# Cross-attention over a long context: a projection in 64-row pieces copied out by two engines, and layer 0's maxima taken over pairs of key blocks with the mask worked into the keys by GpSimd

## The chip, the cores and the metric

The kernel runs on one core of one Trainium2 chip. The time is device microseconds from the start to the end of one execution. Engines are named as in the profile: PE is TensorE's matrix product, PEld its weight load, DVE is VectorE, ACT is ScalarE, POOL is GpSimd, SP is SyncE, which here only issues DMAs.

## The reference

Four layers, each a cross-attention over a context of 12544 tokens of 192 numbers, a self-attention and a feed-forward block of experts, on 128 query tokens of width 256. The change concerns the cross-attentions of layers 0, 1 and 2 (16 heads of 16 numbers; layer 3 has 64 to a head and is written otherwise). Layer 0:

```python
q = (x @ Wq).reshape(B, N, HEADS, hd).transpose(0, 2, 1, 3)
k = (context @ Wk).reshape(B, M, HEADS, hd).transpose(0, 2, 1, 3)
v = (context @ Wv).reshape(B, M, HEADS, hd).transpose(0, 2, 1, 3)
scores = jnp.einsum('bhid,bhjd->bhij', q, k) * scale
scores = jnp.where(context_mask[:, None, None, :], scores, max_neg)
attn = jax.nn.softmax(scores, axis=-1)
out = jnp.einsum('bhij,bhjd->bhid', attn, v)
return out.transpose(0, 2, 1, 3).reshape(B, N, DIM) @ Wo
```

Layers 1 and 2 add biases to q, k and v and have no mask; layer 1 clips the scores at 10000 and replaces the weights by a mean if any score is not a number. All arithmetic is fp32. In the inputs the mask is true everywhere, but the kernel computes with whatever mask it is given.

## The kernel before

The context is cut into 25 blocks of 512 tokens (NSB), the last of 256. Keys and values are projected from it per group `g` of eight heads (two groups in layers 0 to 2), so the context is read once for each group. `Net.context` loads a block ahead: rows 0 to 127 of the transposed context into a tile `ctxA` (128 x 512) and the other 64 rows into `ctxB`, whose two halves of 256 tokens lie in partitions 0 to 63 and 64 to 127.

`Keys.project(g, b, low)` projects block `b` in two parts. With `low` = 0 the products contract over 128 rows (keys: two products of 256 columns, values: four of 128 x 128); with `low` = 1 over the last 64 rows, where the two halves of the block use the upper and the lower half of TensorE's rows. All add into one pair of PSUM banks (`pair`), keys in the first 256 columns of each bank and values in the others. Then ScalarE copies keys (L131, L133 with bias) and values (L137) to SBUF, both halves in one instruction. Each fp32 product appears in the trace as two records of PE and two of PEld. The first blocks of layers 1 and 2 (EARLY = 8) are projected before the layer, while the experts of the layer before run.

`attend_twice_in` goes over the keys twice for each group. The first pass finds the maximum of every query's scores; the second computes exponentials less that maximum and adds up the weighted values. In PSUM there are four pairs of banks (`ppr=4`) that all products of the first pass take in turn, so a product waits until the pair taken four products earlier has been read.

- First pass, layers 1 and 2, "by twos": for blocks 2i and 2i+1, GpSimd makes the difference of the two blocks of keys (`apart`, L570). The scores of the difference go through a relu on ScalarE (`over`, L578), the scores of block 2i+1 are added and the maximum taken by one fused VectorE instruction (`highest_of_two`, L586), since max(a, b) = relu(a - b) + b. A round `b` of the loop does this for one half `s` of the heads' pairs: it projects a block two ahead, makes the scores of the difference, and finishes the maximum of the round before.
- First pass, layer 0 (masked): for each block and `s`, TensorE first writes the mask's row into PSUM by a bf16 product with ones (L558), adds the scores (L559), and VectorE takes the maximum over each bank (`highest`, L565). The mask's rows come into SBUF by four small DMAs a block from SP (L547).
- Second pass: scores (L629), exponentials (L654, L677, L692), weighted values (L699). For layer 0 GpSimd issues four small DMAs of mask rows a block (L547), of which the products read two.

Order: `in_order` binds the instructions of PE, DVE and ACT in a loop to the order in which they are written. GpSimd and SP, whose instructions here are DMAs, differences and sums, are ordered by the scheduler, each in one queue that is worked off in order.

In layer 1 GpSimd also adds up all context columns (`add_up`, L99, L100) for the case of scores that are not numbers. `load_mask` reads the mask and makes its rows and columns. `load_kv` loads a weight of 192 rows: 128 rows once, and the other 64 twice, for both halves of the partitions. The layer-3 attention (`KeysInTurn`, `attend_once_in`) uses the same context tiles with loads two blocks ahead.

Of the kernel before, what the change touches and what calls it, by code (L numbers as in the profile page):

```python
# [12 lines left out]
F32 = mybir.dt.float32  # L13
BF16 = mybir.dt.bfloat16
# [10 lines left out]
CB = CD - P  # L25
H = 16
# [27 lines left out]
class Keys:  # L54
# [4 lines left out]
    def __init__(self, net, wk, wv, groups, bias=None, sums=None):  # L59
        self.net, self.nc, self.wk, self.wv, self.bias, self.sums = net, net.nc, wk, wv, bias, sums  # L60
        self.context = net.context(groups * NSB)
        self.started, self.done, self.rest = {}, 0, None
        if sums is not None:
            self.nc.gpsimd.memset(sums, 0.0)
# [30 lines left out]
    def add_up(self, g, b):  # L95
        if g == 0 and self.sums is not None:
            a, c = self.context(b)
            n = HB * len(self.halves(b))
            self.nc.gpsimd.tensor_tensor(self.sums[:, :n], self.sums[:, :n], a[:, :n], ALU.add)  # L99
            self.nc.gpsimd.tensor_tensor(self.sums[:, SB:], self.sums[:, SB:], c, ALU.add)  # L100
# [16 lines left out]
    def values_into(self, p, g, low, blocks, first=0, turn=None):  # L117
        cols = slice(g * P, g * P + P)
        for j, b in enumerate(blocks):
            ctx = self.context((g if turn is None else turn) * NSB + b)[low]  # L120
            for c in range(2):
                for i, r in self.halves(b):
                    at = first + (2 * j + c) * P
                    r = r if low else slice(0, P)
                    k = c * P if low else i * HB + c * P
                    self.mm(p[:, i, at : at + P], ctx[r, k : k + P], self.wv[r, low, cols], low, first + j + c == 0)

    def keep_keys(self, g, b, p):
        to = self.kT(b).rearrange("p (i k) -> p i k", i=2)[:, : p.shape[1]]
        if self.bias is None:  # L130
            self.nc.scalar.copy(to, p)  # L131
        else:
            self.nc.scalar.activation(to, p, AF.Identity, bias=self.bias[:, g : g + 1])  # L133

    def keep_values(self, g, b, p):
        to = self.v(b).rearrange("p (i c) h e -> p i (c h) e", i=2)[:, : p.shape[1], :, :16]
        self.nc.scalar.copy(to, p.rearrange("p i (h e) -> p i h e", e=16))  # L137

    def steps(self, g):

        todo = [b for b in range(2, NSB) if g * NSB + b >= self.done]
        n, at, out = len(todo), 0, []
        for t in range(NSB):
            to = min(n, -(-n * (t + 1) // (NSB - 2)))
            while to < n and todo[to] <= t + 2:
                to += 1
            out.append([(b, low, b < NSB - 3) for b in todo[at:to] for low in range(2)])
            at = to  # L150
        return out

    def project(self, g, b, low, values=True):


        if g * NSB + b < self.done:
            return
        if not low:
            self.add_up(g, b)
            self.started[g, b] = self.net.early_pair() if self.rest is None else self.net.pair()  # L160
        p = self.started[g, b]
        self.keys_into(p, g, low, [b])
        if values:
            self.values_into(p, g, low, [b], HB)
        if low:
            n = len(self.halves(b))
            self.keep_keys(g, b, p[:, :n, :HB])
            if values:
                self.keep_values(g, b, p[:, :n, HB:])
            self.done = g * NSB + b + 1  # L170

    def project_values(self, g, blocks):
        p = self.net.pair()
        for low in range(2):
            self.values_into(p, g, low, blocks)
        for j, b in enumerate(blocks):
            self.keep_values(g, b, p[:, : len(self.halves(b)), j * HB : (j + 1) * HB])


class KeysInTurn(Keys):  # L180

    def __init__(self, net, wk, wv):
        self.net, self.nc, self.wk, self.wv = net, net.nc, wk, wv
        self.context = net.context((GROUPS3 + 1) * NSB, 2)
        self.first = {}
# [17 lines left out]
class Net:  # L207
    def __init__(self, tc, d, ctx):
        self.tc, self.nc, self.d, self.ctx = tc, tc.nc, d, ctx
        pool = lambda name, bufs, **kw: ctx.enter_context(tc.tile_pool(name=name, bufs=bufs, **kw, reuse_waits="tile"))  # L210
        self.cp = pool("const", 1)
        self.wsp = pool("wsmall", 4)
# [118 lines left out]

    def load_column(self, src, pool, name):
# [50 lines left out]
    def context(self, until, ahead=1):  # L383
# [6 lines left out]
        def get(k):  # L390
            while len(made) <= k + ahead and len(made) < until:
                b = len(made) % NSB
                n = min(SB, S2 - b * SB)
                a = self.ahead.tile([P, SB], F32, tag="ctxA", name="ctxA", bufs=4)
                self.queue.dma_start(a[:, :n], d["ctxA"][:, b * SB : b * SB + n])
                c = self.ahead.tile([P, HB], F32, tag="ctxB", name="ctxB", bufs=4)
                self.queue.dma_start(c, d["ctxB"][b])
                made.append((a, c))
# [4 lines left out]
    def load_mask(self, pool):  # L403
# [3 lines left out]
        m8 = pool.tile([nr, P], U8, tag="m8", name="m8", bufs=1)  # L407
        nc.scalar.dma_start(m8, self.d["mask"])
        mf = pool.tile([nr, P], F32, tag="mf", name="mf", bufs=1)
        nc.vector.tensor_copy(mf, m8)  # L410
        self.ts(mf, mf, 0.0, None, ALU.is_gt)
        some = self.stat(1)
        nc.vector.tensor_reduce(some[:nr], mf, AX.X, ALU.max)
        t = self.tr()
        nc.tensor.transpose(t[:1, 0, :nr], some[:nr], self.ident[:nr, :nr])
        top = self.stat(1)
        nc.vector.tensor_reduce(top[:1], t[:1, 0, :nr], AX.X, ALU.max)
        p = self.ps()
        self.mm(p[:, :1], [(self.ones[:1, :], top[:1])])
        self.any = self.cp.tile([P, 1], F32, tag="any", name="any")  # L420
        nc.vector.tensor_copy(self.any, p[:, :1])
        self.bar = self.cp.tile([P, 1], F32, tag="bar", name="bar")
        self.ts(self.bar, self.any, -NEG, None, ALU.mult)
        m8 = pool.tile([NSB, SB], U8, tag="m8r", name="m8r", bufs=1)
        flat = self.d["mask"].rearrange("c p -> (c p)")
        whole = S2 // SB * SB
        nc.gpsimd.memset(m8, 1)
        nc.scalar.dma_start(m8[: S2 // SB, :], flat[:whole].rearrange("(b k) -> b k", k=SB))
        nc.scalar.dma_start(m8[S2 // SB :, : S2 - whole], flat[whole:].unsqueeze(0))
        self.mask_row = pool.tile([NSB, SB], BF16, tag="maskrow", name="maskrow", bufs=1)  # L430
        self.ts(self.mask_row, m8, 0.0, 1.0, ALU.is_gt, ALU.subtract)
        self.ts(self.mask_row, self.mask_row, self.bar[:NSB], None, ALU.mult)
        self.ts(mf, mf, 1.0, -NEG, ALU.subtract, ALU.mult)
        self.ts(mf, mf, self.any[:nr], None, ALU.mult)
        t = self.tr()
        nc.tensor.transpose(t[:, 0, :nr], mf, self.ident[:nr, :nr])
        self.mask_col = self.cp.tile([P, nr], F32, tag="maskcol", name="maskcol")
# [1473 lines left out]
```

## Time and profile before

| | |
|---|---|
| Median of 3 runs | 3020.04 us (3013.86 to 3021.88) |
| Profiled execution, its own time | 3021.48 us |
| Its span, first to last instruction | 3019.8 us |
| Mean granted TensorE clock | 0.975 |
| Busy: PE, PEld | 2882.8 us (95%), 2209.0 us (73%) |
| Busy: DVE, ACT, POOL | 2024.2 us (67%), 1626.2 us (54%), 282.7 us (9%) |
| First passes, first to last maximum: layer 0, groups 0 and 1 | 22.0 to 162.7 us, 285.3 to 417.1 us |
| First passes: layer 1 | 668.6 to 776.6 us, 920.9 to 1041.7 us |
| First passes: layer 2 | 1322.9 to 1437.4 us, 1568.6 to 1694.0 us |
| Layer 3's cross-attention | about 1865 to 2880 us |

Busy time of an engine is the time that the trace shows it working; PE's is modelled and includes pipelining, so 95% does not mean that TensorE works at its peak. The chain is followed back from the last instruction to whatever released each step. A row of a group gives line, engine, operation, the tiles it writes and reads, its shape and count, then busy time, mean duration in ns, and idle time before it with what ended it. A row of the timeline gives start, duration, engine, line, operation, tiles, shape and count, with idle time before it in brackets. A row of a stretch gives its length and each engine's busy time with its count, then the granted clock, the DMA engines' share and GB/s.

### The profile page before, as it was taken

How to read it: one execution, taken by the hardware profiler on the slowest of the kernel's cores; microseconds unless marked ns; L12 is line 12 of the kernel's file. 1: busy time of each engine (PE TensorE's matmuls, PEld its weight loads, DVE VectorE, ACT ScalarE, POOL GpSimd, SP SyncE). 2: the span in 40 equal slices, each digit the busy share in tenths (PEclk: the TensorE clock that was granted, in tenths of full speed). 3: DMA queues.
4: the chain of work that ended last, by engine and by line, in shares of the span. 5: the costliest groups of instructions: out<-in, count | busy, mean ns of one | idle time of the engine just before them, and what ended most of it. 6: DMA issues, size and time to landing. Idle time of an engine off the chain costs nothing.

```text
span 3019.8 us, 79794 instructions
## 1 busy us (share of the span) xinstructions
PE 2882.8 (95%) x34893; PEld 2209.0 (73%) x34893; DVE 2024.2 (67%) x3241; ACT 1626.2 (54%) x1904; POOL 282.7 (9%) x504
## 2 busy tenths in 40 slices
PE   8999999989999999999999998899999999999969
PEld 5677667455676576765776675688989989889858
DVE  6876887525893598745544555577777777777844
ACT  1176148335685585245875682355655656555521
POOL 7011021223001100211001002000000000000000
PEclk9999999999999999999999998999999999999979
DMA  5201210562002202521012007232322223222436
GB/s 133 61 19 32 72 39 6 189 225 57 21 3 79 59 4 88 175 82 53 15 39 73 23 3 258 92 98 80 85 84 83 85 79 88 85 78 83 136 111 201
DMA packets 177706, 247.28 MB, mean 82 GB/s; under 512 B 32459, under 2 KB 119269, under 8 KB 177358
## 3 DMA queue, kind: packets, MB, share of 16 engines
q1 hardware_dynamic: 165592, 227.26, 24.8%
q0 software_dynamic: 11008, 14.37, 1.6%
q8 instruction: 274, 4.49, 0.6%
q10 hardware_dynamic: 758, 0.55, 0.1%
q14 instruction: 74, 0.61, 0.1%
HBM read 241.56 MB, written 0.13 MB: 80 GB/s over the span
## 4 chain that ended last, share of the span: by engine, by line
PE 83%; DVE 11%; ACT 2%; DMA 1%; issue 1%; SPq 1%; POOL 0%; ACTq 0%; DVEq 0%; POOLq 0%
PE pair L103 21%; PE acc L699 10%; PE pair L559 8%; PE v L103 8%; PE sc L859 6%; PE pair L629 5%; PE acc L901 5%; PE ps L279 5%; PE one L629 4%; DVE parts L565 3%; PE pair L622 2%; PE acc L279 2%; PE kv L103 2%; PE ps L1698 1%; DVE over L586 1%
## 5 line engine op out<-in xcount | busy, mean ns | idle before, releaser
L586 DVE CUSTOM_DVE_ANT_0 over<-over,pair 128x512 f32<-128x512 f32 x384 | 241.2, 683 | 249.2 <-PE pair L559 237.6
L103 PE MATMUL pair<-ctxA,wk 128*128 128x256 f32 x1236 | 328.7, 399 | 6.5 <-ACT over L578 1.8
L103 PEld LDWEIGHTS pair<-ctxA,wk 128*128 128x128 f32 x1236 | 217.0, 190 | 138.5 <-ACT over L578 53.0
L861 ACT COPY kept<-sc 128x1024 f32<-128x1024 f32 (+1 forms) x135 | 136.2, 1009 | 261.2 <-PE sc L859 261.2
L565 DVE TENSOR_REDUCE parts<-pair 128x2 f32<-128x1024 f32 (+1 forms) x216 | 235.7, 1157 | 41.8 <-PE pair L559 41.8
L290 DVE TENSOR_TENSOR top<-top,kept 128x1024 f32<-128x1024 f32 (+2 forms) x145 | 169.1, 1169 | 134.0 <-ACT kept L861 132.7
L293 DVE SCALAR_TENSOR_TENSOR e<-pair,floor 128x1024 f32<-128x1024 f32 x196 | 227.3, 1217 | 14.6 <-PE pair L629 14.6
L677 ACT ACTIVATE e<-pair 128x1024 f32<-128x1024 f32 x196 | 200.7, 1025 | 46.5 <-PE pair L629 26.0
L654 ACT ACTIVATE e<-e 128x1024 f32<-128x1024 f32 x196 | 206.7, 1057 | 35.3 <-DVE e L293 24.3
L629 PE MATMUL pair<-qz,kT 32*128 32x256 f32 x2112 | 218.9, 374 | 0.0
L699 PE MATMUL acc<-e,v 128*17 128x128 f32 x6336 | 211.4, 274 | 3.0 <-ACT e L692 2.2
L699 PEld LDWEIGHTS acc<-e,v 128*17 128x17 f32 x6336 | 155.8, 97 | 67.8 <-ACT e L692 45.6
L692 ACT ACTIVATE e<-e 128x1024 f32<-128x1024 f32 x196 | 205.0, 1048 | 0.0
L293 DVE SCALAR_TENSOR_TENSOR e<-one,maskcol,less 128x256 f32<-128x256 f32 x392 | 162.6, 477 | 53.3 <-PE one L629 43.3
L859 PE MATMUL sc<-qz,kT 64*128 64x128 f32 x2816 | 197.8, 279 | 0.0
L559 PE MATMUL pair<-kT,qz 32*128 32x512 f32 (+1 forms) x1120 | 192.7, 592 | 5.2 <-DVE parts L586 3.8
L578 ACT ACTIVATE over<-pair 128x1024 f32<-128x1024 f32 x192 | 186.9, 1021 | 14.7 <-PE pair L559 7.4
L103 PEld LDWEIGHTS v<-wv,ctxA 128*128 128x128 f32 x1568 | 189.8, 192 | 6.4 <-issue 1.7
L103 PE MATMUL v<-wv,ctxA 128*128 128x128 f32 x1568 | 193.1, 276 | 0.0
L103 PE MATMUL pair<-ctxB,wk 64*128 64x256 f32 x1236 | 188.9, 399 | 0.0
L290 DVE TENSOR_TENSOR e<-one,less 128x512 f32<-128x512 f32 x196 | 126.3, 686 | 88.6 <-PE pair L629 88.1
L859 PEld LDWEIGHTS sc<-qz,kT 64*128 64x128 f32 x2816 | 171.6, 187 | 13.0 <-issue 1.3
(457 smaller groups left out, 5637.7 us busy)
## 6 DMA issues: line engine op xcount, KB each, us to landing
ctxA<-in_ctxA SPq DMA_DIRECT2D x324, 256.0 KB
ctxB<-in_ctxB SPq DMA_DIRECT2D x339, 128.0 KB
w<-in_L_ffn_W SPq DMA_DIRECT2D x32, 1024.0 KB
ctxA<-in_ctxA POOLq DMA_DIRECT2D x36, 256.0 KB, 3.2
w<-in_L_ffn_w_gateT SPq DMA_DIRECT2D x8, 1024.0 KB
wu<-in_L_ffn_w_upT SPq DMA_DIRECT2D x8, 1024.0 KB
w<-in_L_ffn_w_downT SPq DMA_DIRECT2D x8, 1024.0 KB
w<-in_L_ffn_w1T SPq DMA_DIRECT2D x8, 1024.0 KB
```

The lines of the kernel that those rows point to most:

```text
L103: self.nc.tensor.matmul(out, a, b, start=start and not low, stop=low == 1, skip_group_check=True)
L279: self.nc.tensor.matmul(out, lhsT, rhs, start=(i == 0), stop=(i == n - 1))
L290: self.nc.vector.tensor_tensor(out, a, b, op)
L293: self.nc.vector.scalar_tensor_tensor(out, a, s, b, op0, op1, **kw)
L559: nc.tensor.matmul(x, qz[r, g, s, :], k[r, :n], start=not by_mask, stop=True)
L565: nc.vector.tensor_reduce(parts[:, s, 2 * half : 2 * half + 2, i], x, AX.X, ALU.max)
L586: nc.vector.tensor_tensor_reduce(es[half][:, j, :], es[half][:, j, :], x[:, j, :], 1.0, -LARGEST, ALU.add, ALU.max, parts[:, s, 2 * half + ...
L629: nc.tensor.matmul(at, keys.kT(c // 4)[tiles[t], k], q, start=start, stop=True, skip_group_check=True)
L654: nc.scalar.activation(to, to, AF.Exp)
L692: nc.scalar.activation(to, to, AF.Exp)
L699: nc.tensor.matmul(acc[32 * t : 32 * t + 17, half, :], v[:, c % 4 + j, 4 * half + t, :], es[half][:, t // 2, j, t % 2, :], start=c + j + h ...
L859: nc.tensor.matmul(x[:, t, c : c + P], kT[r, c : c + P], qz[r, g, :], start=True, stop=True)
```

## The change

- **Projection.** The context is laid out on the host as 25 blocks of 128 partitions x 768: three chunks of 64 rows, with the first 256 tokens in partitions 0 to 63 and the others in 64 to 127, loaded by one DMA. Weights of layers 0 to 2 lie the same way, twice (`load_twice`). Every product of the projection contracts over 64 rows; the two halves of a block use the two halves of TensorE's rows. Keys come first (part 0), values second (part 1).
- **Copies.** In the passes, half 0 of a block is copied by ScalarE and half 1 by VectorE (`keep`); before a pass, and for blocks whose keys or values are made alone, ScalarE copies both.
- **Layer 0's first pass** is written like that of layers 1 and 2. With v0, v1 the masks of blocks 2i and 2i+1 (1 for a token that counts), GpSimd makes `less[0]` = (a - b) x v0 x v1 and `less[1]` = (a - b) x (v0 - v0 v1) + b, in four operations; a mask row `none` lowers columns where neither counts. The masks come from DRAM, broadcast to 128 partitions (256 KB a pair of blocks); `load_mask` computes them and writes them there. The mask's product (L558) stays for `less[1]` and for the last block.
- **Order.** Layer 0 projects three blocks ahead instead of two (`lead`), so three blocks are projected before each pass.
- **Memory.** Layer 3 takes both parts of a context block from one tile. The space for GpSimd's DMA descriptors is 4096 bytes a partition, set by `dynamic_dma_scratch_size`, where nothing was set.

The core of the diff:

```diff
-        self.context = net.context(groups * NSB)
+        self.context = net.context(groups * NSB, whole=True)
...
+    def keys_into(self, p, g, b):
+        cols = slice(g * P, g * P + P)
+        ctx = self.context(g * NSB + b)
+        for c in range(CH):
+            for i, r in self.halves(b):
+                self.mm(p[:, i, :HB], self.wk[r, c, cols], ctx[r, c, :], c == 0, c == CH - 1)
+
+    def values_into(self, p, g, b, first=0):
+        cols = slice(g * P, g * P + P)
+        ctx = self.context(g * NSB + b)
+        for half in range(2):
+            at = first + half * P
+            for c in range(CH):
+                for i, r in self.halves(b):
+                    self.mm(p[:, i, at : at + P], ctx[r, c, half * P : half * P + P], self.wv[r, c, cols], at + c == 0, c == CH - 1)
+
+    def keep(self, g, b, p):
+        if self.rest is None:
+            self.keep_keys(g, b, p, slice(0, len(self.halves(b))))
+            self.keep_values(g, b, p, slice(0, len(self.halves(b))))
+            return
+        for i, _ in self.halves(b):
+            self.keep_keys(g, b, p, slice(i, i + 1), on_vector=i == 1)
+            self.keep_values(g, b, p, slice(i, i + 1), on_vector=i == 1)
...
+    def project(self, g, b, part, values=True):
+        if g * NSB + b < self.done:
+            return
+        if part == 0:
+            self.add_up(g, b)
+            p = self.started[g, b] = self.net.early_pair() if self.rest is None else self.net.pair()
+            self.keys_into(p, g, b)
+            return
+        p = self.started[g, b]
+        if values:
+            self.values_into(p, g, b, HB)
+            self.keep(g, b, p)
+        else:
+            self.keep_keys(g, b, p, slice(0, len(self.halves(b))))
+        self.done = g * NSB + b + 1
...
+                t = self.ahead.tile([P, SB + HB], F32, tag="ctx", name="ctx", bufs=4)
+                if whole:
+                    self.queue.dma_start(t, d["ctx"][b])
+                    made.append(t.rearrange("p (c k) -> p c k", c=CH))
+                    continue
...
+            m8 = own.tile([np_, 2, SB], U8, tag="m8p", name="m8p", bufs=1)
+            nc.scalar.dma_start(m8, flat[: np_ * 2 * SB].rearrange("(b j k) -> b j k", j=2, k=SB))
+            kept = own.tile([np_, 2, SB], BF16, tag="keptrow", name="keptrow", bufs=1)
+            unless = self.stat(1)
+            self.ts(unless, self.any, -1.0, 1.0, ALU.mult, ALU.add)
+            self.ts(kept, m8, 0.0, unless[:np_], ALU.is_gt, ALU.max)
+            pair = own.tile([np_, 2, SB], BF16, tag="maskpair", name="maskpair", bufs=1)
+            both, first = pair[:, 0], pair[:, 1]
+            self.tt(both, kept[:, 0], kept[:, 1], ALU.mult)
+            self.tt(first, kept[:, 0], both, ALU.subtract)
+            self.mask_pair = self.drp.tile([np_, 2 * SB], BF16, tag="maskpair", name="maskpair")
+            nc.sync.dma_start(self.mask_pair, pair.rearrange("b j k -> b (j k)"))
...
+            valid = pool.tile([P, 2, SB], BF16, tag="valid", name="valid", bufs=2)
+            nc.sync.dma_start(valid.rearrange("p j k -> p (j k)"), self.mask_pair[i : i + 1].to_broadcast([P, 2 * SB]))
+            t = pool.tile([P, 2, SB], F32, tag="apart", name="apart", bufs=2)
+            nc.gpsimd.tensor_tensor(t[:, 0], a, b, ALU.subtract)
+            nc.gpsimd.tensor_tensor(t[:, 1], t[:, 0], valid[:, 1], ALU.mult)
+            nc.gpsimd.tensor_tensor(t[:, 1], t[:, 1], b, ALU.add)
+            nc.gpsimd.tensor_tensor(t[:, 0], t[:, 0], valid[:, 0], ALU.mult)
+            return t[:, 0], t[:, 1], mask_rows(i)
...
+        lead = 3 if masked else 2
...
             for b in range(NSB):
-                if masked:
-                    rows.append(mask_rows(b))
+                i, s = b // 2, b % 2
                 with self.in_order(*engines, before=chain):
                     for step in steps[b]:
                         keys.project(g, *step)
-                    if masked:
+                    es = over(g, i, s, less) if b < NSB - 1 else None
+                    if before is not None:
+                        highest_of_two(g, *before, parts)
+                    if es is not None:
+                        before = i, s, less, es
+                    if b == NSB - 1:
+                        row = mask_rows(b) if masked else None
                         for s in range(2):
-                            highest(g, b, s, parts, b)
-                    else:
...
+                            highest(g, b, s, parts, i, row)
+                    elif s and b < NSB - 2:
+                        less = apart(i + 1)
...
-    nc = bacc.Bacc("TRN2", target_bir_lowering=False, num_devices=1)
+    nc = bacc.Bacc("TRN2", target_bir_lowering=False, num_devices=1, dynamic_dma_scratch_size=4096)
```

## The prediction

> **What bounds the kernel now.** I read the page first (chain and groups), then the busy time by stretch, then inside two of the stretches the chain and the timeline. The page's chain by engine:
>
> ```profile
> PE 83%; DVE 11%; ACT 2%; DMA 1%; issue 1%; SPq 1%; POOL 0%; ACTq 0%; DVEq 0%; POOLq 0%
> ```
>
> TensorE ends the program; GpSimd (POOL) is nowhere on the chain. The change touches the first passes (maxima) over the context in layers 0, 1 and 2. Their stretches (length, PE, PEld, DVE, ACT, POOL, clock, DMA share): layer 0 groups 0 and 1, layer 1 groups 0 and 1.
>
> ```profile
> 22.00:165.00 143.00, 136.83 (x1111) 87.34 (x1109) 114.99 (x110) 23.70 (x46) 46.35 (x97) 0.99 0.31 81
> 284.00:419.00 135.00, 132.46 (x1120) 86.32 (x1118) 114.26 (x105) 24.29 (x47) 7.08 (x10) 1.00 0.23 64
> 662.00:777.00 115.00, 111.83 (x777) 66.10 (x774) 64.54 (x201) 64.39 (x80) 38.83 (x37) 1.00 0.18 51
> 915.00:1042.00 127.00, 124.71 (x900) 80.09 (x894) 63.16 (x197) 70.91 (x92) 16.19 (x15) 0.99 0.24 67
> ```
>
> Layer 0 takes longer and has VectorE 80% busy where layer 1 has it half busy. One round of layer 0 in the chain (start, us, what):
>
> ```profile
> 43.49 3.03 PE pair L103 x24
> 46.52 0.35 PE pair L558 x4
> 46.87 0.87 PE pair L559 x8
> 47.73 0.02 issue
> 47.76 1.24 DVE parts L565
> 49.00 0.04 issue
> 49.04 3.10 PE pair L103 x24
> ```
>
> A round is a ring: project a block (L103), mask product (L558), scores (L559), one VectorE maximum (L565) that frees the oldest of four PSUM pairs, and the next projection takes that pair: 5.62 us. The same round in layer 1's timeline:
>
> ```profile
> 702.75 1.13 PE L103 MATMUL pair<-ctxA,wk 128*128 128x256 f32 x4
> 704.71 0.70 PE L103 MATMUL pair<-ctxB,wk 64*128 64x256 f32 x4
> 705.24 0.61 PE L103 MATMUL pair<-wv,ctxB 64*128 64x128 f32 x8
> 705.78 1.14 PE L559 MATMUL pair<-apart,qz 32*128 32x512 f32 x8
> 705.90 0.69 ACT L133 ACTIVATE kT<-pair,bk 128x512 f32<-128x512 f32 x1 [2.37 <-PE pair L103]
> 706.49 0.58 ACT L137 COPY v<-pair 128x512 f32<-128x512 f32 x1
> 707.01 1.94 ACT L578 ACTIVATE over<-pair 128x1024 f32<-128x1024 f32 x2
> 708.17 0.30 PEld L103 LDWEIGHTS pair<-ctxA,wk 128*128 128x128 f32 x2 [0.76 <-ACT over L578]
> ```
>
> Here ScalarE's first relu (L578) closes the ring: 702.75 to 708.17, 5.42 us, with TensorE idle 0.76 at its end.
>
> **The projection in 64-row pieces.** 6 full-height and 6 half-height products (24 records, fp32 in two) become 18 half-height ones (36 records). Half-height ones run two at a time, so the slots stay: keys 4+2 before, 6 after; values 8+4 before, 12 after. In the timeline a key slot is 0.216 and a value slot 0.111 in either height. What goes is the seam between heights: the value slots before 704.71 take 0.99 for 8 (0.10 too much), and the first key slot after it takes 0.32 instead of 0.216. So 3.03 becomes 0.32 + 5 x 0.216 + 12 x 0.111 + 0.10 (seam to the scores) = 2.83, 0.20 less. Bounds: 3.03 (the seam is only moved) and 2.73 (both seams go).
>
> **Two engines copying.** ScalarE's 0.59 + 0.52 per block falls by a 256-column half each; half rows exist (474 ns with bias beside 687, 372 beside 586), so 0.42 less. But the relu starts at the later of the copies' end (707.01) and the end of its own products (705.78 + 1.14 + 0.05 = 706.97). Only 0.04 us of the 0.42 lies on the ring, and I take 0.02. *The Trainium skill, "TensorEngine Tiling (Array Packing)", section "PSUM Bottleneck", advises draining PSUM with both ScalarE and VectorE; if that saved the full 0.42 in each of 68 rounds the time would be 29 us lower.* The row decides, since the next thing late is the product. VectorE takes two copies of 128x256 (about 0.4 each, the 256-column PSUM copy L285 is 424 ns) after its 2.5 us of maxima: 3.3 of 5.2, hidden; without that cover 0.8 a round.
>
> **Layers 1 and 2.** Ring: 2.83 + 1.19 (products, semaphore) + 1.02 + 0.15 = 5.19, say 5.20 instead of 5.42. Rounds with a full projection: blocks 8 to 21 in group 0 (8 are made early), 2 to 21 in group 1: 34 a layer, 68 in all x 0.22 = 15.0. Keys-only blocks (12) and values-only blocks (18, layer 0's too) each lose a seam, 30 x 0.2 = 6.0; the four blocks projected before group 1, 0.8. Early blocks lie under weight loads (DMA share 0.64 at 532:662): nothing, at most 3.6. Sum -21.8.
>
> **Layer 0, the ring.** The four maxima of 1.22 per round become four fused ones of 0.61 (683 ns, overlapping) and two relus; mask products halve and leave the ring, because the first products of a round read the masked difference. So it is layer 1's ring: 5.20 for 5.62. TensorE's own work is 2.83 + 0.97 + 0.35 + 0.87 = 5.02, just under; a second seam at the mask product would cost up to 0.2 a round. Group 0, from block 5 (43.49) to 21: 17 x 0.42 = 7.1. Group 1: block 2 moves ahead of the pass (P(0) and P(1) there are 6.06 at 272.68), so P(3) starts near 283.5 instead of 286.6, 3.1 earlier; 18 rounds x 0.42 = 7.6; the tail (keys-only at 3.9, bare rounds at 2.6, one extra round of lag) gives 22.6 for 23.8, 1.2. Group 1: -11.9.
>
> **Layer 0, GpSimd's four operations.** Rows:
>
> ```profile
> L547 POOL DMA_DIRECT2D row<-maskrow x200 | 96.5, 487 | 253.3 <-PE pair L672 228.2 <-DMA row<-maskrow 9.3 <-DVE st L1426 8.2
> L570 POOL TENSOR_TENSOR apart<-kT 128x512 f32<-128x512 f32 x32 | 40.7, 1273 | 210.7 <-ACT v L137 148.8 <-PE pair L559 61.9
> ```
>
> Four dependent operations at 1.27 + 0.03 are 5.2 us a pair of blocks, in 10.4 us of rounds. The chain may start when the round 2i has read the tile two pairs back, and must end when round 2i+2 has projected: 5.20 + 2.83 = 8.0 us. It fits, with 2.8 left; only the last pair, with no projection before it, waits about 1.3 (in the tail above). No row multiplies by a bf16 operand; bounds 1.0 (below the row, if half the bytes are cheaper) and 2.5 (twice it); I take 1.27, the same shape and engine. GpSimd's mask DMAs of pass two stand in the same queue: of the 200, 106 are issued before 80 us, the 100 that pass two never reads among them; at 0.49 each they may come between operations, 4 x 1.76 = 7.0, still under 8.0. *The skill's "GPSIMD Engine Reference", section 4.1, gives two-input elementwise work to VectorE as about twice as fast; a VectorE row of this shape is 686 ns.* By that rule the chain were 2.7 us; both are hidden, so the sum is the same.
>
> **Layer 0, the start.** New: a mask load, six small VectorE operations (about 2 us after 16.5), two writes to DRAM, a broadcast read back, GpSimd's last three operations. With 2 to 3 us a transfer (row DMAs on GpSimd's queue land 1.6 to 3.4 after issue) the first difference is ready near 28.4, where scores began at 20.7. TensorE has blocks 2 and 3 to project until 23.6, then waits. But before, VectorE itself stood still 6.4 and 3.7 us there for layer 3's small loads, and steady rounds began at 43.49 with block 5. After: block 4 at 28.4 + 0.9, block 5 near 34.5 (bare ring), or 37 if VectorE's stall to 38.3 returns. I take 37: -6.5; bounds -9 and +3. The new waits stand in two queues: SP waits near 18.5 for VectorE's mask rows, and behind it are the context loads from block 4 on and those small loads; GpSimd waits for the broadcast, and behind it are mask DMAs not needed for 100 us.
>
> **Taken at nothing.** SP's queue: per pair one broadcast and 4 row DMAs instead of 8 rows; one context load a block instead of two. Layer 3's context tile is now freed whole; its loads still go out a step (1015 us / 118 = 8.6) ahead, against 3.2 to land. GpSimd's smaller descriptor space: its issues take 536 to 583 ns, no waits; bounds 0 and +5.
>
> **Sum.** -21.8 - 7.1 - 11.9 - 6.5 = -47.3 against the profiled run's own 3021.48 (span 3019.8; 1.4 over the median 3020.04): 2974.
>
> **Rivals.** (1) *GpSimd becomes layer 0's ring* (slower). Per pair 4x us beyond 8.0 are added; with 24 pairs the gain of 47 is gone at x = 2.5 us an operation; at 2.7 the price is 24 x 2.8 = 67, time 3041. For: unseen bf16 form, DMA issues in its queue. Against: 1.27 in every GpSimd row of this shape (1262 to 1280), beside VectorE's fused maxima. 0.15. (2) *Half the gain*: the seam stays (layers 1 and 2 give 3), or group 0's start and queue eat layer 0's: 2995. For: the start is the least known. 0.15. (3) *The copies do count*, the relu follows the copies because VectorE's half is early and products shrink too: 29 more, 2945. Against: 706.97. 0.05. (4) *Gains and losses cancel*, 3011 to 3029: 0.05. The forecast's own case, 2955 to 2990: 0.60.
>
> **How the numbers follow.** A change under 0.3% (9 us) can't be told from none. Faster: 0.60 + 0.15 + 0.05 = 0.80; same 0.05; slower 0.15. The range reaches from 2945 (rival 3; the forecast's own case ends at 2955: start at -9, early blocks, half the second seam) to 3005 (rival 2 with some of GpSimd's excess), and leaves out rivals 1 and 4, 0.20.
>
> **What would show it.** Projection pieces of 36 records in 2.83 us; rounds of 5.20 in all three layers, closed by the relu; L565's line left with 24 small reductions; first scores near 28 us; four GpSimd operations of 1.27 a pair, seldom waited for. Wrong if scores in layer 0 wait for the difference in every second round, if a projection still takes 3.0, or if layer 3 moves.

## The result, and the profile after

The changed kernel takes 3098.38 us (median of 4 runs, 3090.45 to 3108.92) where the kernel before took 3017.36 beside it: a ratio of 1.027, 95% interval 1.0235 to 1.0305. It is slower. The forecast was 2974, with 2945 to 3005 as its range. The profiled run is 3098.43 with a span of 3096.4.

The four stretches that were shown of before, as the changed kernel runs them (window, length, PE, PEld, DVE, ACT, POOL busy, granted clock, DMA share and rate): layer 0 groups 0 and 1, layer 1 groups 0 and 1.

```profile
41.00:213.00 172.00, 129.39 (x1224) 82.07 (x1221) 78.59 (x241) 59.26 (x89) 96.85 (x136) 0.89 0.25 71
334.00:470.00 136.00, 130.35 (x1246) 83.26 (x1242) 78.15 (x239) 61.54 (x93) 58.32 (x50) 1.00 0.27 83
710.00:833.00 123.00, 115.73 (x958) 67.39 (x950) 76.77 (x232) 59.87 (x83) 37.37 (x24) 0.99 0.17 51
971.00:1106.00 135.00, 132.62 (x1174) 82.34 (x1166) 80.33 (x242) 64.01 (x94) 15.62 (x14) 0.99 0.22 67
```

Two things stand out. In layer 0's first group TensorE is busy 129 of 172 us where it was 137 of 143, and GpSimd 97 us where it was 46. And layer 1, where only the projection and its copies were changed, has become longer as well. The page's chain by engine still names TensorE first; its shares add up to 74% because it could not be followed back to the start, so for layer 0 it is no help and the waits are.

```profile
PE 64%; DVE 6%; ACT 2%; issue 1%; POOL 1%; DMA 0%; DVEq 0%; POOLq 0%; SPq 0%; ACTq 0%
```

**Layer 0, group 0: 45 of the 77 us.** What TensorE waited for up to 210 us (total, times, longest):

```profile
PE pair L628 <- POOL apart L649: 44.6, 5, 21.8
```

L628 are the first products of a pair of blocks, L649 the last of the four operations on GpSimd. GpSimd's own timeline in the longest of these waits (start, length, what; a row "x33" is 33 issues in a run):

```profile
63.22 15.70 POOL L617 DMA_DIRECT2D row<-maskrow  x33 [0.78 <-DMA row<-maskrow]
78.93 1.27 POOL L646 TENSOR_TENSOR apart<-kv 128x512 f32<-128x512 f32 x1
80.14 0.52 POOL L617 DMA_DIRECT2D row<-maskrow  x1
80.68 1.16 POOL L647 TENSOR_TENSOR apart<-apart,valid 128x512 f32<-128x512 f32 x1
81.78 0.55 POOL L617 DMA_DIRECT2D row<-maskrow  x1
82.35 1.27 POOL L648 TENSOR_TENSOR apart<-apart,kv 128x512 f32<-128x512 f32 x1
83.57 1.15 POOL L649 TENSOR_TENSOR apart<-apart,valid 128x512 f32<-128x512 f32 x1
```

The four operations take 4.9 us, near the forecast. In front of them stand 33 row loads for pass two, nearly all of rows that no product reads: the trace has 106 such loads before 103 us, and of a row's four loads two are read, in three buffers, so at most 6 of the 106 are for rows that are read. The other 100 are the unread ones of both groups. TensorE has nothing to do meanwhile, and its granted clock falls to half and needs a few microseconds after the work is back (same columns as above, 6 us a window):

```profile
62.00:68.00 6.00, 0.97 (x18) 0.78 (x14) 0.77 (x4) 0.65 (x2) 5.22 (x12) 1.00 0.03 2
68.00:74.00 6.00, 0.00 (x0) 0.00 (x0) 0.00 (x0) 0.00 (x0) 6.00 (x13) 0.50 0.04 2
80.00:86.00 6.00, 1.22 (x8) 0.68 (x12) 0.00 (x0) 0.00 (x0) 5.96 (x9) 0.50 0.03 6
86.00:92.00 6.00, 6.00 (x59) 3.60 (x52) 2.52 (x8) 2.28 (x4) 3.76 (x9) 0.80 0.62 173
```

The account of the group, from the starts of the projections: block 5 starts at 41.7 (43.4 before), three steps between projections take 12.7, 28.6 and 18.1 instead of 5.7 (42.4 too much), the other rounds 5.67 and 5.72 instead of 5.62 (1.3), and the tail from the first keys-only block on 27.1 instead of 23.8 (3.3): -1.7 + 42.4 + 1.3 + 3.3 = 45.3. By the ends of the first passes, the other 31 us come as 4.5 in layer 0's group 1, 12 in layer 1, 14 in layer 2 (8 of them between layers 1 and 2, see the clock below) and 1 after it.

**Layers 1 and 2: a longer round.** One round of layer 1's group 1, to be held against the one of before:

```profile
988.64 1.57 PE L101 MATMUL pair<-ctx,wk 64*128 64x256 f32 x12
990.04 1.50 PE L101 MATMUL pair<-wv,ctx 64*128 64x128 f32 x24
991.47 1.14 PE L628 MATMUL pair<-apart,qz 32*128 32x512 f32 x8
991.59 0.48 ACT L142 ACTIVATE kv<-pair,bk 128x256 f32<-128x256 f32 x1 [2.69 <-PE pair L101]
991.96 0.37 ACT L150 COPY kv<-pair 128x256 f32<-128x256 f32 x1
992.36 0.48 DVE L138 TENSOR_SCALAR kv<-pair,bk 128x256 f32<-128x256 f32 x1 [2.07 <-ACT kv L150]
992.70 1.94 ACT L657 ACTIVATE over<-pair 128x1024 f32<-128x1024 f32 x2 [0.37 <-ACT kv L150]
992.76 0.41 DVE L148 COPY kv<-pair 128x256 f32<-128x256 f32 x1
993.29 0.33 PEld L628 LDWEIGHTS pair<-kv,qz 32*128 32x128 f32 x4 [0.66 <-issue]
994.38 1.17 PEld L101 LDWEIGHTS pair<-ctx,wk 64*128 64x128 f32 x12 [0.76 <-ACT over L657]
```

The projection takes 988.64 to 991.47, 2.83 us, as forecast. But VectorE's first copy waits for ScalarE's last one (the bracket at 992.36), so the four half copies run in series and end at 993.17, 1.70 us after the projection; the two whole ones of before ended after 1.28. The second products' last two tiles are written into the pair that these copies empty, so their weights are loaded only at 993.29, and the next projection follows them: 994.38. The ring is 2.83 (projection) + 0.12 + 0.77 (ScalarE) + 0.81 (VectorE) + 0.12 + 1.09 (from these weights to the next projection) = 5.74 us, where 5.42 stood before and 5.20 was forecast.

### The profile page after: what moved, and what is told of

It is laid out like the page before. It is cut to its first block, busy times and chain, and to the rows that moved or that the text cites. A ratio compares the mean times of both kernels' runs of the same rounds, so it can differ in the third digit from the quotient of the medians.

```text
span 3096.4 us, 83195 instructions
## 1 busy us (share of the span) xinstructions
PE 2914.6 (94%) x36469; PEld 2210.5 (71%) x36469; DVE 2012.6 (65%) x3666; ACT 1673.0 (54%) x2000; POOL 385.0 (12%) x556
## 4 chain that ended last, share of the span: by engine, by line
PE 64%; DVE 6%; ACT 2%; issue 1%; POOL 1%; DMA 0%; DVEq 0%; POOLq 0%; SPq 0%; ACTq 0%
PE v L203 8%; PE pair L203 7%; PE pair L101 7%; PE acc L778 6%; PE pair L628 6%; PE sc L934 6%; PE acc L976 6%; PE pair L708 4%; PE ps L317 3%; PE pair L701 2%; PE acc L317 2%; PE one L708 1%; DVE over L665 1%; PE kv L101 1%; PE ps L1772 1%
## 5 line engine op out<-in xcount | busy, mean ns | idle before, releaser
L665 DVE CUSTOM_DVE_ANT_0 over<-over,pair 128x512 f32<-128x512 f32 x576 | 361.9, 684 | 148.5 <-PE pair L628 138.3
L628 PE MATMUL pair<-apart,qz 32*128 32x512 f32 x1536 | 264.3, 643 | 53.9 <-POOL apart L649 48.0
L203 PEld LDWEIGHTS v<-wv,ctx 64*128 64x128 f32 (+1 forms) x3136 | 296.0, 190 | 12.2 <-issue 1.9
L203 PE MATMUL v<-wv,ctx 64*128 64x128 f32 (+1 forms) x3136 | 301.2, 275 | 0.0
L203 PE MATMUL pair<-ctx,wk 64*128 64x256 f32 (+1 forms) x1440 | 276.0, 384 | 1.2 <-ACT kT L231 1.1
L756 ACT ACTIVATE e<-pair 128x1024 f32<-128x1024 f32 x196 | 200.5, 1024 | 48.9 <-PE pair L708 26.3
L101 PEld LDWEIGHTS pair<-ctx,wk 64*128 64x128 f32 x1548 | 143.5, 188 | 109.2 <-ACT over L657 84.7
L203 PEld LDWEIGHTS pair<-ctx,wk 64*128 64x128 f32 (+1 forms) x1440 | 192.3, 188 | 34.1 <-issue 13.2
L101 PEld LDWEIGHTS pair<-wv,ctx 64*128 64x128 f32 x3096 | 204.2, 193 | 12.1 <-ACT over L657 3.0
L101 PE MATMUL pair<-ctx,wk 64*128 64x256 f32 x1548 | 208.9, 397 | 2.6 <-ACT over L657 1.7
L101 PE MATMUL pair<-wv,ctx 64*128 64x128 f32 x3096 | 206.5, 278 | 0.0
```

The source lines that it names most:

```text
L101: self.nc.tensor.matmul(out, a, b, start=first, stop=last, skip_group_check=True)
L203: self.nc.tensor.matmul(out, a, b, start=start and not low, stop=low == 1, skip_group_check=True)
L628: nc.tensor.matmul(x, qz[r, g, s, :], k[r, :n], start=row is None, stop=True)
L665: nc.vector.tensor_tensor_reduce(es[half][:, j, :], es[half][:, j, :], x[:, j, :], 1.0, -LARGEST, ALU.add, ALU.max, parts[:, s, 2 * half + ...
L756: nc.scalar.activation(to, pair, AF.Exp)
```

## The experiments

Two theories came out of this. Q: the row loads of pass two stand in front of work that pass one waits for. S: the two engines' copies run in series and put the pair back later. First and last maximum and the ring in the tables are read from each trace; times are medians, with the ratio to the kernel before in the same session (3017.36 beside the changed kernel, 3023.18 beside E1 to E4).

### Each cause alone, and both

E1: pass two loads the mask rows of the two tiles that read them.

```diff
-            for t in range(4):
+            for t in range(2 if second else 4):
```

> The changed kernel, with pass two of layer 0 loading its mask rows only for the two tiles whose products read them (50 row DMAs a group instead of 100); the output is the same. Theory Q (the queue): in group 0 the differences stood behind runs of row DMAs on GpSimd, two stalls of 27 and 17 us; without the unread half the runs are half as long or gone, and the first pass of group 0 ends 25 to 45 us earlier: 3055 to 3073. Rival C (the chain itself is too long: mask pairs through DRAM, broadcast, four operations): the stalls stay, 3090 or more. Layers 1 and 2 do not move in either.

E2: ScalarE keeps a block's keys and VectorE its values.

```diff
-        for i, _ in self.halves(b):
-            self.keep_keys(g, b, p, slice(i, i + 1), on_vector=i == 1)
-            self.keep_values(g, b, p, slice(i, i + 1), on_vector=i == 1)
+        every = slice(0, len(self.halves(b)))
+        self.keep_keys(g, b, p, every)
+        self.keep_values(g, b, p, every, on_vector=True)
```

> The changed kernel, but ScalarE copies a block's keys (both halves) and VectorE its values (both halves). Theory S (the copies stand in series: VectorE's first starts 0.03 us after ScalarE's last, and the second products' last two tiles wait for VectorE's last): if VectorE no longer waits, the ring of layers 1 and 2 falls from 5.74 to about 5.22, the time by about 68 x 0.52 + 12 in layer 0 = 47; if two readers of one PSUM tile are still put one after the other, copies end 0.69 + 0.03 + 0.58 after their start instead of 1.58, the ring is about 5.46, the time 68 x 0.28 + 8 = 27 lower, 3071. Rival V (the ring is longer because VectorE now has copies ahead of its maxima): no change, 3098.

E3: ScalarE copies all.

```diff
-        self.keep_values(g, b, p, every, on_vector=True)
+        self.keep_values(g, b, p, every)
```

> The changed kernel with the copies back on ScalarE alone, as before the change; projection in 64-row pieces and layer 0 by twos stay. Theory S: copies end 1.16 us after they start instead of 1.58, then the relu closes the ring: 5.22 in layers 1 and 2, 68 x 0.52 = 35 lower, and layer 0 group 1 about 5.3 instead of 5.8, another 9: 3054. Rival H (half-height products make the ring longer): layers 1 and 2 stay at 5.6 or more, 3085 to 3098.

E4: E1 and E3 together.

> The two edits together: only the read mask rows, and copies on ScalarE alone. Theories Q and S: they act in different places, except in group 0 of layer 0, so the sum, 3098 - 35 - 44 = about 3010 to 3025, near the kernel before; the late start of layer 0 (19 us) and some 8 us between layers 1 and 2 are left. If one cause stands behind both: not lower than the better of the two.

| kernel | us | ratio to before (interval) | layer 0 group 0, first to last maximum | ring, layer 0 group 1 | ring, layers 1 and 2 |
|---|---|---|---|---|---|
| before | 3023.18 | | 22.0 to 162.7 | 5.62 | 5.42 |
| changed | 3098.38 | 1.027 (1.0235 to 1.0305) | 41.4 to 207.9 | 5.78, 5.83 | 5.74 |
| E1 | 3058.47 | 1.0122 (1.0105 to 1.014) | 41.3 to 165.2 | 5.78, 5.83 | 5.74 |
| E2 | 3075.43 | 1.0179 (1.0156 to 1.0202) | 41.5 to 203.4 | 5.55 | 5.47 |
| E3 | 3063.99 | 1.0142 (1.0121 to 1.0163) | 40.9 to 201.6 | 5.32 | 5.22 |
| E4 | 3027.00 | 1.0008 (0.999 to 1.0025) | 41.4 to 157.4 | 5.31, 5.32 | 5.22 |

E1 takes the three stalls away; TensorE is busy 121 of the 124 us again:

```profile
41.00:165.00 124.00, 121.05 (x1162) 78.14 (x1162) 75.27 (x230) 56.47 (x83) 48.11 (x40) 1.00 0.30 90
```

Rival C is out. E2 shows what VectorE waits for. There ScalarE writes only the keys tile and VectorE only the values tile; what they share is the PSUM pair, and VectorE still begins when ScalarE has ended (2.43 and 1.76 are the idle times before):

```profile
993.26 0.69 ACT L142 ACTIVATE kv<-pair,bk 128x512 f32<-128x512 f32 x1 [2.43 <-PE pair L101]
...
993.98 0.69 DVE L148 COPY kv<-pair 128x512 f32<-128x512 f32 x1 [1.76 <-ACT kv L142]
```

Its ring of 5.47 is the 5.46 that was worked out for two readers put one after the other. E3 brings the forecast's ring, 5.22, with the relu closing it again; the copies end 987.78 - 986.50 = 1.28 after the projection as before the change, and the weights follow at once:

```profile
986.50 1.14 PE L628 MATMUL pair<-apart,qz 32*128 32x512 f32 x8
...
986.62 0.69 ACT L142 ACTIVATE kv<-pair,bk 128x512 f32<-128x512 f32 x1 [2.18 <-PE pair L101]
...
987.20 0.58 ACT L150 COPY kv<-pair 128x512 f32<-128x512 f32 x1
...
987.83 0.30 PEld L628 LDWEIGHTS pair<-kv,qz 32*128 32x128 f32 x4 [0.17 <-ACT kv L150]
...
988.89 1.17 PEld L101 LDWEIGHTS pair<-ctx,wk 64*128 64x128 f32 x12 [0.76 <-ACT over L657]
```

So VectorE's maxima, which come after its copies, are not what lengthened the ring, and neither are the half-height products: rival V is out by E2, whose one copy on VectorE is 0.12 us shorter than the two halves while the ring fell by 0.27, and rival H by E3. E3's time fell by 34 where 44 was expected. E4's 71 is close to the sum of the two (40 + 34); by the ratios, which take out the 6 us between the sessions, it is 79 against 45 + 39. Both theories hold, and yet E4 only draws level with before.

### Is it the place in the queue, or the number of loads?

E5: the kernel before, with E1's edit.

> The kernel before the change with the one edit of the first experiment: pass two loads its mask rows only for the two tiles that read them. Theory Q says the row DMAs hurt only because something that TensorE needs stands behind them on GpSimd; in layer 0 before the change nothing does: no change, within 5 us of the kernel before. Rival D (the row DMAs load the DMA engines and slow whatever runs beside them): 10 us or more faster.

E6: all four rows, issued by SyncE in both passes.

```diff
-                (nc.gpsimd if second else nc.sync).dma_start(row[at + 32 * t : at + 32 * t + 1, :n], src)
+                nc.sync.dma_start(row[at + 32 * t : at + 32 * t + 1, :n], src)
```

> The changed kernel with all four mask rows of pass two kept, but issued by SyncE instead of GpSimd. Theory Q: the differences no longer stand behind them, the two stalls of group 0 go, and the time falls by about as much as in the first experiment (3058), unless SyncE's own loads of context blocks and mask pairs now come late behind the rows (then 3060 to 3085). Rival D (it is the number of DMAs, not the queue): 3090 or more.

E9: all four rows on GpSimd, with its order written out.

```diff
-                        less = apart(i + 1)
+                        with self.in_order(mybir.EngineType.Pool, before=queued):
+                            less = apart(i + 1)
...
-                        rows.append(mask_rows(c // 4, True))
+                        with self.in_order(mybir.EngineType.Pool, before=queued):
+                            rows.append(mask_rows(c // 4, True))
```

> The changed kernel with all four mask rows of pass two kept and issued by GpSimd as before, but the order of GpSimd's queue written out: pass two's row DMAs stand behind all twelve differences of their group. Theory Q (what costs is the place of the rows in front of work that pass one waits for, on whichever queue): the stalls of group 0 go and the time is that of the first experiment or a little less, since nothing stands between the first differences either: 3050 to 3060; all four rows are then issued while pass two runs, and PE waits there are small because a row is needed only every 9 us. Rival D (the number of row DMAs): 3085 or more, or the same loss moved into pass two.

E5 gave 3026.48, 1.0009 of before (0.9994 to 1.0025): before the change the same loads cost nothing. E6 was a miss: 3096.09, no better. GpSimd is now nearly free of blame, but the loads went to the head of SyncE's queue in the same way (24 in a run from 38.9 us, 17.5 us long), and what stands behind them there are pass one's own mask rows (TensorE's waits up to 210 us):

```profile
PE pair L627 <- DMA row<-masknone: 24.9, 3, 12.6
...
PE pair L628 <- POOL apart L649: 5.6, 2, 4.3
```

E6 alone would have fitted rival D, the mere number of loads. E9 settles it: the same 100 loads a group on the same engine, but behind the differences, give 3053.95 (1.011, 1.0092 to 1.0128), a little under E1, with this left of the waits up to 170 us:

```profile
PE pair L628 <- POOL apart L649: 4.2, 2, 2.9
```

It is the place in an in-order queue. That the unread half went so far ahead fits the rest: a row that a product reads can't be loaded again before that product, and one that nobody reads has no such brake. E1 shows the brake: it keeps the read half unordered, issues 6 of these loads by 33.5 us and the next at 170.75, after a wait for a product, and has no long stall.

### Where the rest of the forecast gain went

E7: E4 with the mask left out of the keys (layer 0's first pass then has no exact mask on single keys; one subtraction is left of the four operations).

```diff
-            if not masked:
+            if True:
                 less = pool.tile([P, SB], F32, tag="late", name="apart", bufs=3)
                 nc.gpsimd.tensor_tensor(less, a, b, ALU.subtract)
-                return less, b, None
+                return less, b, mask_rows(i) if masked else None
```

> The fourth experiment's kernel (only the read rows, copies on ScalarE), with the mask left out of the keys: the difference is one subtraction, no mask pair is waited for, and the first pass of layer 0 computes maxima without the exact mask on single keys (blocks where both are masked still get the row). It prices the mask chain itself. If the late start of layer 0 (first maximum at 41 us where it was 22) and the waits at the end of its passes (1.3 and 2.7 us) come from the four operations and the mask pair's way through memory, first maximum near 30 and some 10 to 18 lower than the fourth experiment; if they come from the weights, context loads and the extra round of lag, no more than 5 lower.

E8: E4 with layer 0's maxima block by block, as before the change; the mask pairs are not made.

```diff
-        lead = 3 if masked else 2
+        lead = 2
...
+                if masked:
+                    rows.append(mask_rows(b))
...
+                    if masked:
+                        for s in range(2):
+                            highest(g, b, s, parts, b, rows[-1])
-                    es = over(g, i, s, less) if b < NSB - 1 else None
+                    es = over(g, i, s, less) if b < NSB - 1 and not masked else None
```

> The fourth experiment's kernel with layer 0's maxima taken block by block with the mask row, as before the change: what is left of the change is the projection in 64-row pieces. By the rings (0.2 a round in layer 0, 0.2 in layers 1 and 2: 37 + 68 rounds) 21 under the kernel before, 2999. Theory G (layer 0 by twos gives its ring's gain back at its start and at the ends of its passes): within 8 us of the fourth experiment. Rival: by twos is worth its 25 us there, and this is 25 slower than the fourth.

E7 gave 3004.01 (0.9943 of before, 0.9922 to 0.9963). The first maximum came at 34.7 instead of 41.4, not at 30, the tails shrank from 27.1 and 29.6 to 26.4 and 26.3, and layer 0's rounds were 5.26 throughout. So the mask chain costs layer 0 some 7 us at its start and 4 in its tails; the remaining 2.6 over the old tail of 23.8 go with the extra round of lag by twos. These 11 us are half of the 23 between E7 and E4; E7's runs also have a higher clock, 0.974 on average for E4's 0.970 (see below). E8 gave 3022.17 (1.0008, 0.9993 to 1.0023), 5 under E4 and the same by the ratio: theory G holds within what can be told. With the 64-row projection alone the ring is 0.20 shorter in all three layers (5.42 and 5.22), the 21 us of the expectation, and the time does not move. Its trace shows two places where 14 us of it went: block 5 is projected at 50.3 instead of 43.4, and the first pass of layer 1's group 0 takes 113.9 instead of 107.3; it takes 112.8 to 116.2 in every kernel with the new projection.

E10: E4 with E9's order and the adding up of the context in two operations.

```diff
-            self.nc.gpsimd.tensor_tensor(self.sums, self.sums, self.context(b), ALU.add)
+            for at in (slice(0, SB), slice(SB, SB + HB)):
+                self.nc.gpsimd.tensor_tensor(flat[:, at], flat[:, at], ctx[:, at], ALU.add)
```

> The fourth experiment's kernel (only the read rows, copies on ScalarE) with two more edits: GpSimd's row DMAs behind the differences, and layer 1's adding up of the context in two operations of 512 and 256 columns as before the change instead of one of 768. Expected: first maximum of layer 0 about 2 us earlier (39 for 41), the two-round steps of layer 1's group 0 back from 9.8 to about 8.6 (four of them: 5 us); together 5 to 8 under the fourth experiment, 3019 to 3022, if the merged addition is what the differences wait for in layer 1; if it is the context load that it waits for, only 2.

E11: E10 with each context block loaded in three DMAs.

```diff
-                    self.queue.dma_start(t, d["ctx"][b])
+                    for c in range(CH):
+                        at = slice(c * HB, c * HB + HB)
+                        self.queue.dma_start(t[:, at], d["ctx"][b][:, at])
```

> The tenth experiment's kernel with every context block of layers 0 to 2 loaded in three DMAs of 256 columns instead of one of 768. If layer 0's first projection is late because a whole block of 393 KB must land (PE waits 5.9 us for it at the start), the start comes 3 to 6 us earlier; if the DMA engines are simply full there, nothing, or a little slower by the two extra issues a block (0.35 us each on SyncE's queue, not on the path).

They gave 3020.80 (0.9998, 0.9983 to 1.0014) and 3022.01 (0.9997, 0.9983 to 1.0011). E10's first maximum came 1.9 earlier, as expected from the order. Its steps of two rounds in layer 1's group 0 stayed at 9.6 to 10.1 (8.8 before the change), so it isn't the addition's being one operation. The chain of E10 there:

```profile
679.81 2.01 PE pair L104 x30
681.82 0.02 SPq L444
681.84 0.04 issue
681.88 2.94 DMA ctx<-in_ctx
...
686.18 0.74 POOL sums L101
686.91 1.24 POOL apart L644
688.15 0.04 issue
688.19 2.07 PE pair L631 x16
```

A context load goes out when a projection has given its buffer back, the addition waits for that load, and the difference stands behind the addition on GpSimd, with TensorE waiting for it. E11 changed this step little (9.5), and its first maximum, at 41.2, came 1.7 later than E10's instead of 3 to 6 earlier.

E12: E4 with E9's order and context blocks loaded two ahead.

```diff
-        self.context = net.context(groups * NSB, whole=True)
+        self.context = net.context(groups * NSB, 2, whole=True)
```

> The fourth experiment's kernel with GpSimd's row DMAs behind the differences (as in the tenth) and, in layers 0 to 2, context blocks loaded two ahead instead of one (the addition of the context as one operation). In the tenth's chain a step of two rounds in layer 1's group 0 runs from a context load over the addition and the difference to the first products. If the load's lateness sets it, those steps fall from 9.9 to about 8.6, the first pass of that group from 115 to about 110, and the time by 5 against the tenth; if the place of the addition in GpSimd's queue sets it, they stay. Layer 0's start may come a little earlier too. Against the kernel before: 6 to 12 lower at the same granted clock, which is barely over what can be told.

E12 gave 3012.68, 0.9965 of before (0.9946 to 0.9983): 9 us under the kernel before, hardly more than can be told. The steps it was made for stayed at 9.8, so by its expectation it is the addition's place in GpSimd's queue that sets them; its chain still runs from a load (2.97 us) over the addition (1.82) and the difference (1.23) to the products. Layer 2, which has no addition, agrees: there the step is 8.61 in E4, E8, E10 and E12 (8.80 before), and E4's pass of its group 0 is 1.6 shorter than before. What is new in layer 1 is when the load goes out: before the change, `ctxA` was given back when the 128-row products had read it (one projection starts at 702.75, the load goes at 704.84); the one tile is given back at the projection's end (in E4 700.44 and 703.37). No run moved the addition behind the difference.

**The clock.** E4's 10 runs lie from 3012.22, at a mean granted clock of 0.974, to 3033.41 at 0.966, 2.4 us for each 0.001 by a line through all ten; E8, E10, E11 and E12 give 1.9 to 2.8. At 0.974 the runs of before in E12's session take 3018 to 3022, E4's 3012 and 3014, E12's 3013.5. At the same clock E4 and E12 are thus, by these few runs, some 8 us faster than before; but E4 runs at 0.970 on the average, before at 0.974 and E12 at 0.974. The changed kernel's own profile has a dip of the clock between layers 1 and 2, where early blocks are projected between other work, and the time from layer 1's last maximum to layer 2's first is 289.6 us instead of 281.9:

```profile
1276.00:1280.00 4.00, 4.00 (x25) 3.32 (x24) 2.98 (x6) 0.63 (x1) 0.00 (x0) 0.50 0.00 0
...
1288.00:1292.00 4.00, 4.00 (x20) 3.31 (x20) 0.68 (x3) 0.76 (x2) 0.00 (x0) 0.50 0.00 0
```

TensorE is busy throughout these windows and has half its clock all the same, for some 25 us, with no gap over 1.3 us in it and two stretches of 10 us (1272.5 to 1282.9, 1284.1 to 1294.8) with none. What brings such dips about more often in one kernel than in another was not settled.

## Why the prediction was wrong

**Projection, 2.83 us.** Right, to the last digit.

**Two engines copying.** This step failed. It took 0.42 off ScalarE and called VectorE's half hidden, and looked only at VectorE's load (3.3 of 5.2 us). It didn't ask when VectorE may begin. The copies' end, the thing that frees the pair, moved from 1.28 to 1.70 after the projection instead of forward. In place of 15.0 gained in 68 full rounds stand 68 x 0.32 = 21.8 lost, an estimate. Rival 3 had the copies count, but the other way. The prediction weighed the Trainium skill's "TensorEngine Tiling (Array Packing)", section "PSUM Bottleneck", which advises both engines; the row decided against a gain, but neither that section nor the step spoke of order. The skill's "PSUM — Partial Sum Buffer", section "PSUM bank collisions raise a hardware error", bears on it: two engines must not be in one bank at the same time, and may be in different banks. By it E2's wait is needed, since both engines read both banks; the changed kernel's halves lie in a bank each, and its program waits all the same. No run here shows two engines copying at once; the halves in two PSUM tiles would be the trial, and no run has it.

**Layers 1 and 2, ring 5.20.** Right for ScalarE's copies (5.22). The 0.2 for a block with keys or values only shows too where E4 can be held against before: in layer 1's group 1 a keys-only round takes 3.80 for 3.99, a values-only projection 1.54 for 1.73, and the pass is 4.0 shorter, 18 full rounds x 0.20 and two keys-only ones.

**Layer 0, GpSimd's queue.** The step that cost most. It counted 106 row loads before 80 us, and then let one come between two operations, "4 x 1.76 = 7.0, still under 8.0". They came in runs, 33 in front of one difference, 15.7 us against a slack of 8.0. The operations themselves were right: 4.9 for 5.2. Rival 1 had the right engine and named the queue's issues, but its price was a longer operation; nothing in the sum priced a run of loads. The right question was in the prediction's own count: 100 loads x 0.49 = 49 us of issues are due before 80 us, and the new work stands behind them.

**The start.** First products at 32.2 for 28.4, block 5 at 41.7 for 37: the gain was 1.7, not 6.5. **The rings of layer 0** were 5.26 (group 0) and 5.32 (group 1) in E4, for 5.20, inside the bound; E7 has 5.26 in both, with the mask products still in it, so the 0.06 in group 1 goes with the four operations and the mask pair. **The tails** were forecast at 22.6 and came out at 27.1 and 29.0.

**Taken at nothing:** one context load a block instead of two. Its tile is given back later, and in layer 1's group 0 the addition, with the difference behind it, comes late by about 1 us a step; the pass is 6 longer.

**The clock** was not in the sum at all. The stalls drew it down: the skill's "TensorE: Matmul & The Clock Gate", Part 1, has it at half after an idle window of about 3.4 us and full again after a busy one, and the windows above agree: 0.50 at 68 to 86 us, 0.80 in the first 6 us of work. The dip between layers 1 and 2 does not agree: there the clock stayed at 0.50 through two stretches of 10 us without a gap.

## What to carry to other kernels

When work is put on an engine, list everything that stands in that engine's in-order queue at that time, DMA issues too, and assume that a load with no reader to hold it back is issued as early as it can be; here moving the loads to another queue moved the stall with them, and a written order or fewer loads took it away. When an evacuation is shared between two engines, ask first whether the second may begin before the first has ended, and price the end of the last copy, not each engine's load. And a shorter ring is worth its rounds only where the start, the tails and the other users of its buffers keep up: here 21 us of rings gave nothing in E8.

## What the runs showed of the hardware that was not expected

GpSimd's product with a bf16 operand (L647) is shorter than a product of the same shape with both operands in fp32 (L1706), not longer (columns: count, busy, mean ns, idle before):

```profile
L647 POOL TENSOR_TENSOR apart<-apart,valid 128x512 f32<-128x512 f32 x24 | 27.8, 1157 | 3.1 <-DMA row<-masknone 1.4
L1706 POOL TENSOR_TENSOR s<-s,pre 128x512 f32<-128x512 f32 x16 | 20.3, 1268 | 53.7 <-DVE s L337 39.0 <-DVE probs L328 14.7
```

A row load issued by GpSimd takes its queue 0.48 us each, 33 of them 15.7 us. And a run's time goes with its mean granted clock, 1.9 to 2.8 us for each 0.001: 21 us over the spread of E4's runs, nearly as much as the edits of E2 or E7 are worth.
